# Packing the two parities of a projection as 128 + 64 columns, in a four-layer convolution and scan kernel

## The chip, the cores and the metric

The kernel runs on one core of one Trainium2 chip. The metric is device time in microseconds (us) of one execution. Engines are named as in the profile: PE is TensorE's matrix unit and PEld its weight loads, DVE is VectorE, ACT is ScalarE, POOL is GpSimd, and SP is SyncE, which only issues DMAs.

## The reference

64 images of 96 channels and 28 x 28 pixels go through four layers in float32. Layer 0 is an inverted residual block whose kernels are mixed from four experts by routing weights of the image, with a squeeze-and-excite gate; layers 1 and 3 are plain inverted residual blocks; layer 2 is a selective scan over four quadrants of the image.

```python
# layer 0
rw = softmax(relu(pool @ r_w1.T + r_b1) @ r_w2.T + r_b2)
out = silu(_bn(einsum('oc,bchw->bohw', exp_w, x), ...))            # 96 -> 576 channels
out = silu(_bn(_dwconv_per_sample(out, einsum('be,eckl->bckl', rw, dw_w)), ...))   # 5 x 5
sc = sigmoid(silu(out.mean(axis=(2, 3)) @ se_w1.T + se_b1) @ se_w2.T + se_b2)
out = out * sc[:, :, None, None]
out = einsum('boc,bchw->bohw', einsum('be,eoc->boc', rw, pw_w), out)   # 576 -> 96
x = x + _bn(out, ...)
# layers 1 and 3
out = relu(_bn(_conv(x, w1), ...))                                 # 96 -> 576
out = relu(_bn(_conv(out, wd, stride=1, padding=1, groups=M), ...))    # 3 x 3
x = _bn(_conv(out, w3), ...) + x                                   # 576 -> 96
# layer 2, for each of four quadrants: norm, 1x1 conv, 3x3 depthwise conv, then four scans
h = dA * h + (d_t * u_t)[..., None] * B_t[:, :, None, :]           # 196 steps
y_t = einsum('bdcn,bdn->bdc', h, C_t)
```

## The kernel before

**Stages.** In the steady part four images are in work: one in layer 2 (`mamba`), the others in layers 1, 0 and 3 (`convs`). `slot` sets up one step of this pipeline for each image, `opening` and the end of `mk_conv_seq_kernel` the ramps.

**A convolution block** has three parts. `expand` (L725, L755) multiplies the image by 4.5 blocks of 128 hidden channels; ScalarE evicts each bank into one of two padded tiles, `border` (L709), and stores it in HBM (`ex`). `load` fetches shifted rows of `ex` into `rep`, with SyncE's DMAs, and builds or fetches the taps `wd`. `depthwise` (L835) does the depthwise convolution on PE as a small matmul per column offset, in column tiles of 32; a partition of its result holds one hidden channel at one parity of the image row: 4 blocks x 2 parities x 16 channels, so 64 hidden channels on 128 partitions. ScalarE evicts it into an `acc` tile of 128 partitions and 392 elements (14 row pairs x 28), L845. A projection needs nine `acc` tiles ("groups") for 576 channels.

**`project`** (L872) multiplies the nine `acc` tiles by the projection weights. An `acc` tile holds both row parities on its partitions, so the weights of parity `o` are zero on the partitions of the other parity: for each group, two matmuls of 128 partitions x 96 columns run over the same 392 elements, one into each of two PSUM banks. VectorE adds bias and residual (L876). For layers 1 and 3 the weights are constants (`w3` in the blob); for layer 0 `squeeze_excite` mixes them on PE (L969) and VectorE multiplies them by the gate into `wp` (L994), once for each parity. Nine groups are three operations of six matmuls each.

**Layer 2.** `head` normalises a half image (`group_norm`: statistics on VectorE, small matmuls L1075, L1071 and L1072 on PE, small operations on ScalarE and GpSimd), then shifted matmuls (L1119), taps (L1141) and two 1x1 convolutions (L1162, L1173). `scans` does, for each of 12 scan pairs of an image, on ScalarE the decays (L1269) and a copy of the inputs into `du` (L1279), on VectorE two products (L1291) and two scans in each direction (L1296, L1301), on GpSimd four sums and products (L1248). L1223 sums the states on PE. `tail` normalises, gates and adds.

**The order.** Nothing runs when it is written down: `Plan.op` records each operation with its engine, an estimated cost, what it reads and writes and a due time. `Plan.run` simulates the engines and, on each, always takes the candidate of the earliest due time among those that could start first; an operation may start at most `AHEAD` (45 us) before its due time. The due time is a position on a time axis on which one image takes `T` = 145 us, plus a correction from the table `DUE` for each kind of operation. The instructions are then emitted in that order, and each engine works strictly in it. Where the plan sees PE idle so long that its clock would fall, `idle` puts filler matmuls on zeros (L539) ahead of the next one. The pools (`POOLS`) hold 4 PSUM banks `ps`, 12 `acc` tiles and one `du`.

Of the kernel before, what the change touches and what calls it, by code (L numbers as in the profile page):

```python
# [10 lines left out]
AF = mybir.ActivationFunctionType  # L11
# [143 lines left out]
def pack_l1(ins, layer):  # L155
# [12 lines left out]
    out = np.zeros((4, 2, CB, 2, NG, C), np.float32)  # L168
    for o in range(2):
        out[:, o, :, o] = w3.reshape(4, 2, CB, NG, C)[:, o]  # L170
    p.add("w3", out.reshape(P, 2 * NG, C))
# [4 lines left out]
def pack_l2(ins):  # L176
# [41 lines left out]
PE, ACT, DVE, POOL, SP = "PE", "ACT", "DVE", "POOL", "SP"  # L218
EXP, PLUS, SILU = "exp", "plus", "silu"
# [11 lines left out]
    71, -2, 48, -17, 58, 181, 21, -12, 9, -37, -2, 21, 37, -23, 1, -16, 19, -12, 30, -17, 33, -40, 12, -8, -30, -60,  # L231
    -12, 9, 0, -16, 16, -56, 115, 47, -23, -9, 16, 45, -29, 63, -28, 34, 12, 35, 43, 2, -32, -7, 21, -7, 6, 14, 37,
    13, -22, 36, -19, 13, -27, 7, -23, -17, 130, -19, 113, 50, 16, 35, 28, 2, 22, 11, -45, 12, -30, 30, -30, -13, -6,
    -6, -12, -8, -7, 20, 24, 117, 11, 25, -20, 15, -13, 1, 51, 43, 29, 147, 47, 40, -10, -15, -7, 10, 30, -10, 20,
    129, 8, 11, 31,
# [17 lines left out]
class Plan:  # L253
# [4 lines left out]
    AHEAD = 45.0  # L258

    HOP = {PE: 1.0, DVE: 0.6, ACT: 0.4, POOL: 0.4, SP: 0.2}  # L260
    LAND = 0.7
    ALONE = 130e3
    RATE = 300e3
    TABLE = 1.28
    ANY_ORDER = ("ps", "gs")
    WARM, WINDOW = 0.7, 3.4
    GRACE = {PE: 0.3, ACT: 0.2, DVE: 0.25, POOL: 0.25, SP: 0.0}
# [10 lines left out]
    def op(self, engine, cost, fn, r=(), w=(), due=None, table=None, nbytes=0, after=(), land=None, lock=False):  # L278
        o = Op()
        o.engine, o.cost, o.fn, o.table, o.nbytes = engine, cost, fn, table, nbytes  # L280
        o.land, o.lock = land, lock or engine == POOL
        kind = self.k.kinds.setdefault((fn.__code__, self.tag), len(self.k.kinds))
        o.due = (self.due if due is None else due) + (DUE[kind] if kind < len(DUE) else 0.0)
# [39 lines left out]
    def run(self, start=0.0):  # L323
# [3 lines left out]
        table, dma, left, lock, ahead = None, start, len(self.ops), start, None  # L327
        used = []
# [18 lines left out]
        while left:  # L347
            best = None
            for e, q in queue.items():
# [16 lines left out]
                key = lambda c: (c[1].due + (8.0 if c[1].table and c[1].table != table else 0.0), c[1].n)  # L366
# [9 lines left out]
            if o.table and o.table != table:  # L376
                cost += self.TABLE
                table = o.table
# [11 lines left out]
            o.behind = None  # L390
# [7 lines left out]
            if o.nbytes:  # L398

                dma = max(dma, t + 0.5) + o.nbytes / self.RATE  # L400
                end = max(dma + 1.5, t + cost + (o.land or 2.0 + o.nbytes / self.ALONE)) + self.LAND
# [6 lines left out]
            for b in set(o.bufs):  # L408
                b.left -= 1
                b.end = max(b.end, end + 0.2)  # L410
            for d, data in o.out:
                d.wait -= 1
                if data:
                    d.ready = max(d.ready, end + (self.HOP[d.engine] if d.engine != e or o.nbytes else 0.0))
                if not d.wait:
                    queue[d.engine].append(d)
# [56 lines left out]
class Kernel:  # L473
    T = 145.0
# [13 lines left out]
        wp=(1, [P, 2, NG, C]),  # L488
# [90 lines left out]
    def fold_bn3(self, row, w3):  # L579

        k = w3.shape[1]
        self.nc.vector.tensor_tensor(w3, w3, row.rearrange("p (a o) -> p a o", a=1).to_broadcast([P, k, C]), ALU.mult)
# [12 lines left out]
    def setup(self, fold, banks):  # L595
# [22 lines left out]
        for layer, c in ((1, c1), (3, c3)):  # L618
# [4 lines left out]
            self.fold_bn3(self.row_of(banks, s3, eye, f"fold_row{layer}"), c("w3"))  # L623
# [75 lines left out]
    def expand(self, d):  # L699
# [17 lines left out]
        for t in range(4):  # L717
# [3 lines left out]
            for h in range(2):  # L721
                ps = pl.buf("ps")

                def mm(ps=ps, t=t, h=h):
# [4 lines left out]
                pl.op(PE, 0.72, mm, r=d["keys"], w=[ps], after=[("pad", i, h)])  # L729
                pl.op(  # L730
                    ACT, 0.68, lambda ps=ps, t=t, h=h, pad=pad: evict(pad[:, :, 1 + 7 * h : 8 + 7 * h, 2:30], ps, t),
# [38 lines left out]
        pl.op(PE, 0.81, mm, r=d["keys"], w=[ps], after=["hpad"])  # L770
        pl.op(ACT, 0.68, lambda: evict(pad[:, :, :, 2:30], ps, 4), r=[ps], w=["hpad"], table=d["table"])
# [14 lines left out]
    def load(self, d, u):  # L786
# [18 lines left out]
        if layer == 0:  # L805
            pl.op(POOL, 1.3, spread, r=[d["kern"]], w=[wd])
# [713 lines left out]
```

## Time and profile before

| what | value |
|---|---|
| median of 3 runs | 9315.91 us (9309.75 to 9317.01) |
| the profiled execution | 9312.17 us |
| its span | 9310.4 us |
| mean granted PE clock | 0.965 |
| ACT busy | 6345.8 us |
| POOL busy | 6778.1 us |
| DMA moved | 2029.93 MB, mean 218 GB/s |

The profile's groups name the line, the engine, the operation, the tile that is written and those that are read; behind "x" is the count, then come the busy time in us, the mean time of one in ns, and the idle time of the engine just before them with what ended it. "128*96" ahead of a shape is rows by columns of the PE array that a matmul uses. A float32 matmul is recorded as two matmuls and two weight loads. PE's matmuls are pipelined, so the time of one in a run is read from start to start.

### The profile page before, as it was taken

What the parts mean: (1) busy time and instruction counts of PE and PEld (TensorE: products, weight loads), DVE (VectorE), ACT (ScalarE), POOL (GpSimd) and SP (SyncE); (2) the same over time, 40 slices, a digit from 0 to 9 for tenths busy, and PEclk for the clock granted to TensorE, in tenths of its full rate; (3) what the DMA queues carried; (4) which work ended last, traced back from release to release, by engine and by line L of the source; (5) the groups of instructions that cost most, each with busy time, mean ns of one, the idle gap of its engine ahead of it and who ended that gap; (6) DMA issues with size and microseconds to landing.
All of it is one profiled execution on the core that took longest, in us unless ns stands there. A gap on an engine that the chain in (4) does not pass through costs nothing. (4 is left out here: it accounts for less than half of the span.)

```text
span 9310.4 us, 198515 instructions
## 1 busy us (share of the span) xinstructions
PE 8870.7 (95%) x78114; PEld 4120.6 (44%) x78114; DVE 7772.0 (83%) x7806; ACT 6345.8 (68%) x10934; POOL 6778.1 (73%) x4445
## 2 busy tenths in 40 slices
PE   7899999999999999999999999999999999999997
PEld 3344444444444444444444444444444444444443
DVE  1888888888888888888888888888888888888886
ACT  3667767767667677667677676676676676776763
POOL 2777777777777777777777777777777777777775
PEclk9899999999999999999999999999999999999998
DMA  6688888888888888888888888888888888888884
GB/s 174 185 213 231 223 220 225 227 222 220 224 226 219 221 229 221 215 229 224 219 225 227 223 222 225 224 220 222 228 221 222 227 222 215 230 223 220 225 227 105
DMA packets 1063983, 2029.93 MB, mean 218 GB/s; under 512 B 114065, under 2 KB 890001, under 8 KB 1062673
## 3 DMA queue, kind: packets, MB, share of 16 engines
q1 hardware_dynamic: 810576, 1520.44, 66.6%
q10 hardware_dynamic: 252480, 496.79, 15.4%
q8 instruction: 624, 10.22, 0.5%
q14 instruction: 303, 2.47, 0.1%
HBM read 1499.83 MB, written 516.95 MB: 217 GB/s over the span
## 5 line engine op out<-in xcount | busy, mean ns | idle before, releaser
L835 PE MATMUL ps<-rep,wd 64*32 64x392 f32 (+1 forms) x50688 | 3609.0, 521 | 38.8 <-DMA rep<-ex 14.9
L1301 DVE TENSOR_TENSOR_SCAN g<-decay,b 128x788 f32<-128x788 f32 x1536 | 2755.1, 1794 | 324.8 <-ACT decay L1269 190.1
L1296 DVE TENSOR_TENSOR_SCAN h<-decay,b 128x788 f32<-128x788 f32 x1536 | 2721.4, 1772 | 0.0
L835 PEld LDWEIGHTS ps<-rep,wd 64*32 64x32 f32 (+1 forms) x50688 | 1491.4, 110 | 1822.9 <-issue 1596.4
L1248 POOL TENSOR_TENSOR yc<-h,g 128x784 f32<-128x784 f32 x768 | 1436.9, 1871 | 1095.9 <-DVE h L1296 657.6
L1291 DVE TENSOR_TENSOR b<-du,B 128x784 f32<-128x784 f32 x1536 | 1505.0, 980 | 675.9 <-ACT du L1279 605.8
L845 ACT ACTIVATE acc<-ps,l_bn2b,l_bn2s 128x392 f32<-128x392 f32 x1728 | 1124.2, 674 | 1338.1 <-PE ps L835 1311.3
L1248 POOL TENSOR_TENSOR g<-h,g 128x784 f32<-128x784 f32 x768 | 1425.7, 1856 | 801.4 <-DVE h L1296 800.6
L872 PE MATMUL ps<-acc,blob 128*96 128x392 f32 x4608 | 1602.3, 498 | 4.7
L1248 POOL TENSOR_TENSOR yc<-yc,C 128x784 f32<-128x784 f32 x768 | 1426.5, 1857 | 55.2
L1269 ACT ACTIVATE decay<-dd,A 128x784 f32<-128x784 f32 x1536 | 1372.5, 943 | 38.0 <-DVE h L1296 14.4
L1248 POOL TENSOR_TENSOR yc<-yc,g 128x784 f32<-128x784 f32 x768 | 1318.1, 1716 | 45.9
L725 PE MATMUL ps<-x,blob 96*128 96x392 f32 x3072 | 1186.5, 518 | 22.3 <-ACT border L709 9.5
L709 ACT ACTIVATE border<-ps,l_bn1b,l_bn1s 128x392 f32<-128x392 f32 x1536 | 976.0, 677 | 220.0 <-DMA ex<-border 109.1
L872 PEld LDWEIGHTS ps<-acc,blob 128*96 128x96 f32 x4608 | 725.8, 163 | 755.8 <-issue 635.3
L588 POOL TENSOR_TENSOR wd<-kern,blob 96x640 f32<-96x640 f32 x576 | 753.6, 1317 | 163.1 <-PE ps L835 85.1
L1269 ACT ACT_TABLE_LOAD x439 | 563.2, 1283 | 334.7 <-issue 178.6
L725 PEld LDWEIGHTS ps<-x,blob 96*128 96x128 f32 x3072 | 536.7, 191 | 547.5 <-ACT acc L845 79.7
L872 PE MATMUL ps<-acc,wp 128*96 128x392 f32 x2304 | 771.8, 493 | 0.6 <-ACT a L1166 0.6
L872 PEld LDWEIGHTS ps<-acc,wp 128*96 128x96 f32 x2304 | 376.4, 163 | 383.7 <-issue 373.6
L1279 ACT COPY du<-dd 128x392 f32<-128x392 f32 x768 | 374.2, 487 | 219.0 <-DVE b L1291 124.3
L1223 PE MATMUL y<-yc,blob 128*32 128x392 f32 x3072 | 398.1, 502 | 29.8 <-POOL yc L1248 29.8
(144 smaller groups left out, 6599.8 us busy)
## 6 DMA issues: line engine op xcount, KB each, us to landing
rep<-ex SPq DMA_DIRECT2D x4032, 224.0 KB, 5.1
ex<-border ACTq DMA_DIRECT2D x512, 480.0 KB, 5.5
dd<-ddd SPq DMA_DIRECT2D x384, 588.0 KB, 7.2
ex<-border ACTq DMA_DIRECT2D x256, 512.0 KB, 5.1
B<-bcd SPq DMA_DIRECT2D x256, 392.0 KB, 4.3
C<-bcd SPq DMA_DIRECT2D x256, 392.0 KB, 4.8
wd<-taps SPq DMA_DIRECT2D x512, 192.0 KB, 6.7
ddd<-dd ACTq DMA_DIRECT2D x128, 441.0 KB, 3.5
```

The lines of the kernel that those rows point to most:

```text
L588: self.nc.gpsimd.tensor_tensor(out, taps.rearrange("k (n a) -> k n a", a=1).to_broadcast([k, n, cb]), mask.rearrange("k (a c) -> k a c", a ...
L709: nc.scalar.activation(dst, ps()[:, :HALF].rearrange("p (r o w) -> p o r w", o=2, w=28), d["func"], bias=bias[:, t : t + 1], scale=scale[: ...
L725: nc.tensor.matmul(ps()[:, :HALF], w1[:, t * P : t * P + P], x[:, h * HALF : (h + 1) * HALF], start=True, stop=True)
L835: nc.tensor.matmul(ps()[32 * b : 32 * b + 32, :HALF], wd()[64 * h : 64 * h + lanes, at : at + 2 * CB], rep()[64 * h : 64 * h + lanes, b, : ...
L845: nc.scalar.activation(acc(), ps()[:, :HALF], d["func"], bias=bias[:, at : at + 1], scale=scale[:, at : at + 1], **kw)
L872: nc.tensor.matmul(banks[o]()[:C, :HALF], w, a, start=(g == 0), stop=(g == NG - 1))
L1223: nc.tensor.matmul(y()[32 * j : 32 * j + 32, :HALF], c("sel"), ys[j]()[:, 2 * u : 2 * u + 2], start=(k == 0 and u == 0), stop=(k == 1 and ...
L1248: nc.gpsimd.tensor_tensor(*vs, op)
L1269: nc.scalar.activation(fs[:, :, u, :, :SEQ], d()[:, :2].rearrange("p o (i l) -> p o i l", i=2), AF.Exp, scale=self.A[:, at : at + 1],)
L1291: nc.vector.tensor_tensor(out, v, w, ALU.mult)
L1296: lambda h=h, ff=ff: nc.vector.tensor_tensor_scan(flat(h()), ff, b, 0.0, ALU.mult, ALU.add),
L1301: lambda g=g, ff=ff: nc.vector.tensor_tensor_scan(flat(g())[:, ::-1], ff[:, ::-1], b[:, ::-1], 0.0, ALU.mult, ALU.add),
```

## The change

**Weights.** Of each group, the 96 columns of parity 0 and 32 columns (channels 64 to 95) of parity 1 are packed side by side into 128 columns; the other 64 columns of parity 1 (channels 0 to 63) form a second part. `w3` and `wp` have the shape [128, 9, 192] now, in place of [128, 18, 96] and [128, 2, 9, 96].

**Matmuls.** Three groups give one operation of three 128-column matmuls over 392 elements into bank 0, and one operation of six matmuls of 64 columns over 196 elements into bank 1: the lower 64 array columns take the first half of the elements, the upper 64 the second half.

**Additions.** The two additions become four, after both parts: parity 0 (96 partitions), channels 64 to 95 of parity 1 (32 partitions), and twice 64 partitions by 196 elements. The gate of layer 0 and the setup's fold of the scale are split in the same way.

**The plan.** PE's operations have a form, `FULL` or `TILED`; a change of form costs `MODE` (0.1 us) in the plan and counts 0.5 in the choice among candidates. `AHEAD` goes from 45 to 500, `T` from 145 to 134, `DUE` is a new table, many estimated costs are a little lower, times are rounded to 1/256 us, and a small lag after an operation (`LAG`) is counted.

```diff
@@ pack_l1
-    out = np.zeros((4, 2, CB, 2, NG, C), np.float32)
-    for o in range(2):
-        out[:, o, :, o] = w3.reshape(4, 2, CB, NG, C)[:, o]
-    p.add("w3", out.reshape(P, 2 * NG, C))
+    w3 = w3.reshape(4, 2, CB, NG, C)
+    out = np.zeros((4, 2, CB, NG, 2 * C), np.float32)
+    out[:, 0, :, :, :C] = w3[:, 0]
+    out[:, 1, :, :, C:P] = w3[:, 1, :, :, 64:]
+    out[:, 1, :, :, P:] = w3[:, 1, :, :, :64]
+    p.add("w3", out.reshape(P, NG, 2 * C))
@@ Plan
-    AHEAD = 45.0
+    AHEAD = 500.0
+    LAG = {PE: 0.0, DVE: tick(0.1), ACT: tick(0.1), POOL: tick(0.05), SP: 0.0}
-    TABLE = 1.28
+    TABLE, MODE = tick(1.28), tick(0.1)
+    MODE_PEN = 0.5
@@ Plan.op
+        o.table = table or (FULL if engine == PE else None)
@@ Plan.run
-                key = lambda c: (c[1].due + (8.0 if c[1].table and c[1].table != table else 0.0), c[1].n)
+                other = lambda o: o.table and o.table != (mode if o.engine == PE else table)
+                key = lambda c: (c[1].due + (self.MODE_PEN if e == PE else 8.0) * bool(other(c[1])), c[1].n)
...
-            if o.table and o.table != table:
-                cost += self.TABLE
-                table = o.table
+            if other(o):
+                if e == PE:
+                    cost += self.MODE
+                    mode = o.table
+                else:
+                    cost += self.TABLE
+                    table = o.table
@@ Kernel
-    T = 145.0
+    T = 134.0
-        wp=(1, [P, 2, NG, C]),
+        wp=(1, [P, NG, 2 * C]),
@@ setup
-            self.fold_bn3(self.row_of(banks, s3, eye, f"fold_row{layer}"), c("w3"))
+            row = self.row_of(banks, s3, eye, f"fold_row{layer}")
+            for lo, hi, out in ((0, C, 0), (64, C, C), (0, 64, P)):
+                self.fold_bn3(row[:, lo:hi], c("w3")[:, :, out : out + hi - lo])
@@ depthwise
-        pl.op(PE, 0.69 * k, mm, r=[rep, wd], w=[*banks, *accs])
+        pl.op(PE, 0.67 * k, mm, r=[rep, wd], w=[*banks, *accs], table=TILED)
@@ project
-        def mm(lo):
+        def mm(half, lo):
             for g in range(lo, lo + 3):
-                for o in range(2):
-                    w, a = terms(o, g)
-                    nc.tensor.matmul(banks[o]()[:C, :HALF], w, a, start=(g == 0), stop=(g == NG - 1))
-
-        def add(o):
-            xs = d["x"].rearrange("c (r o w) -> c o r w", o=2, w=28)[:, o]
+                w, a, kw = weights()[:, g], accs[g](), dict(start=(g == 0), stop=(g == NG - 1))
+                if half == 0:
+                    nc.tensor.matmul(banks[0]()[:, :HALF], w[:, :P], a, **kw)
+                    continue
+                for h in range(2):
+                    nc.tensor.matmul(
+                        banks[1]()[64 * h : 64 * h + 64, :SEQ], w[:, P:], a[:, h * SEQ : h * SEQ + SEQ], **kw
+                    )
+
+        xs = lambda o: d["x"].rearrange("c (r o w) -> c o r w", o=2, w=28)[:, o]
+
+        def add(x, ps, lo, hi):
             nc.vector.scalar_tensor_tensor(
-                xs, banks[o]()[:C, :HALF].rearrange("c (r w) -> c r w", w=28), d["b3"], xs, ALU.add, ALU.add
+                x, ps.rearrange("c (r w) -> c r w", w=28), d["b3"][lo:hi], x, ALU.add, ALU.add
             )
 
+        def first():
+            add(xs(0), banks[0]()[:C, :HALF], 0, C)
+            add(xs(1)[64:], banks[0]()[C:, :HALF], 64, C)
+
+        def second():
+            for h in range(2):
+                add(xs(1)[:64, 7 * h : 7 * h + 7], banks[1]()[64 * h : 64 * h + 64, :SEQ], 0, 64)
+
         for lo in range(0, NG, 3):
-            pl.op(PE, 0.67 * 6, lambda lo=lo: mm(lo), r=[*(accs[lo : lo + 3] if lo else accs), wp], w=banks)
-        for o in range(2):
-            pl.op(DVE, 0.65, lambda o=o: add(o), r=[banks[o], *d["keys"]], w=d["keys"])
+            ready = [*(accs[lo : lo + 3] if lo else accs), wp]
+            pl.op(PE, 1.97, lambda lo=lo: mm(0, lo), r=ready, w=[banks[0]])
+            pl.op(PE, 1.27, lambda lo=lo: mm(1, lo), r=ready, w=[banks[1]], table=TILED)
+        pl.op(DVE, 1.3, first, r=[banks[0], *d["keys"]], w=d["keys"])
+        pl.op(DVE, 0.78, second, r=[banks[1], *d["keys"]], w=d["keys"])
@@ squeeze_excite
+            def gated(o, lo=lo, hi=hi, acc=acc):
+                for a, b, out in ((0, C, 0),) if o == 0 else ((64, C, C), (0, 64, P)):
+                    v = sc()[:, o * NG + lo : o * NG + hi].rearrange("p (g a) -> p g a", a=1)
+                    nc.vector.tensor_tensor(
+                        wp()[:, lo:hi, out : out + b - a], acc()[:, :, a:b], v.to_broadcast([P, hi - lo, b - a]), ALU.mult
+                    )
```

## The prediction

> **What bounds the kernel now.** I read the page first, then one image's stretch by windows, then TensorE's timeline inside it.
>
> The page, with its groups of instructions:
>
> ```profile
> span 9310.4 us, 198515 instructions
> ...
> PE 8870.7 (95%) x78114; PEld 4120.6 (44%) x78114; DVE 7772.0 (83%) x7806; ACT 6345.8 (68%) x10934; POOL 6778.1 (73%) x4445
> ...
> L872 PE MATMUL ps<-acc,blob 128*96 128x392 f32 x4608 | 1602.3, 498 | 4.7
> ...
> L872 PE MATMUL ps<-acc,wp 128*96 128x392 f32 x2304 | 771.8, 493 | 0.6 <-ACT a L1166 0.6
> ```
>
> PE is busy 95% of the span, and the projections (L872) are a quarter of that. A float32 matmul leaves two records, so 4608 + 2304 records are 3456 matmuls: 192 projections (64 images, three layers) of 9 groups and 2 parities.
>
> One image by windows (length; busy time of PE, PEld, DVE, ACT, POOL; granted clock; DMA share; GB/s):
>
> ```profile
> 4000.00:4141.00 141.00, 136.09 (x1213) 63.30 (x1215) 119.10 (x117) 98.56 (x171) 104.10 (x70) 0.96 0.84 221
> 4052.00:4057.00 5.00, 0.77 (x4) 0.39 (x2) 3.25 (x2) 2.81 (x4) 0.00 (x0) 0.89 0.63 226
> 4057.00:4070.00 13.00, 12.90 (x135) 7.66 (x134) 9.95 (x12) 8.66 (x20) 9.96 (x9) 0.65 0.89 235
> ```
>
> PE works 136 of 141 us, VectorE (DVE) 119. The five missing us stand in one place, 4052 to 4057, and the 13 us after it run at a clock of 0.65. TensorE's timeline (start, length, group) shows the place, and the prices that I use:
>
> ```profile
> 4025.34 2.17 PE L1141 MATMUL ps<-p,blob 128*32 128x196 f32 x36
> 4027.43 0.90 PE L1162 MATMUL ps<-hn,blob 96*96 96x392 f32 x2
> ...
> 4029.02 12.02 PE L872 MATMUL ps<-acc,wp 128*96 128x392 f32 x36
> 4040.97 4.27 PE L835 MATMUL ps<-rep,wd 64*32 64x392 f32 x96
> 4045.17 2.90 PE L725 MATMUL ps<-x,blob 96*128 96x392 f32 x8
> 4048.00 1.52 PE L1223 MATMUL y<-yc,blob 128*32 128x392 f32 x12
> 4049.45 2.90 PE L725 MATMUL ps<-x,blob 96*128 96x392 f32 x8
> 4056.58 0.48 PE L1075 MATMUL ps<-gs,blob 96*96 96x2 f32 x2 [4.23 <-ACT border L709]
> ...
> 4098.13 0.88 PE L755 MATMUL ps<-x,blob 96*64 96x392 f32 x4
> 4098.94 2.96 PE L725 MATMUL ps<-x,blob 96*128 96x392 f32 x8
> ```
>
> A burst of eight expansions (L725) fills the banks, ScalarE cannot evict into `border`, and the small L1075 stands for 4.23 us. The table of waits (total, times, longest) gives its total, and VectorE's longest wait; the page's chain of waits covers the last 100 us alone, so I leave it:
>
> ```profile
> DVE b L1291 <- ACT du L1279: 605.8, 181, 14.0
> ...
> PE ps L1075 <- ACT border L709: 226.8, 61, 5.4
> ```
>
> The stall comes 61 times in 64 images. With the mean clock of 0.965, at most 0.035 x 9310.4 = 326 us of PE time is lost to the low clock; the stall and what follows it are worth up to 226.8 + 326 = 553 us.
>
> **The projection itself.** Removed: 3456 full-height matmuls of 96 columns. One costs (4040.97 - 4029.02) / 18 = 0.664 us, so 2295 us. Added: 1728 matmuls of 128 columns over the same 392 elements, and 1728 pairs of 64-column tiles, each over 196. The first stream as many elements and cost 0.664: 1147 us. L725 has 128 columns: 4 in 4048.00 - 4045.17 = 2.83, 0.708 each with the edges of so short a run in it; that is the upper bound (1223 us). For the pair the nearest row is L1141: three column tiles side by side, 196 elements, six rounds in 4027.43 - 4025.34 = 2.09 us, 0.348 a round. Two tiles abreast for the same stream: 1728 x 0.348 = 601 us. That tiles of 64 columns run side by side is shown by L755: two matmuls over 392 from 4098.13 to 4098.94, 0.81 us, where one after the other would take 1.33.
>
> Bounds of the pair: half a full matmul, 0.332, from below; from above its four weight loads one behind the other. L755's loads have a median of 136 ns, so 0.544 a pair, 940 us. I take 0.348, because L1141 issues 36 loads of 109 ns, 3.9 us in all, within its 2.09, so loads do overlap.
>
> [...]
>
> **Changes of array form.** In the order of the built programs, changes between full width, 64 and 32 columns go from 2440 to 2809. Price: L755's 0.81 less 0.664, shared by entering and leaving, 0.073; 369 x 0.073 = 27 us. Bounds 0 and 0.146 (54 us).
>
> Sum of this part: 2295 - 1147 - 601 - 27 = 520 us less; between 78 (2295 - 1223 - 940 - 54) and 574 (2295 - 1147 - 574).
>
> **VectorE's part.** Two additions of 96x392 (L876, 226.6 us over 384, some 0.6 each) become four: 96x392, 32x392 (as many elements a partition, so again 0.6) and two of 64x196, for which the nearest rows are L1358 (0.345) and L1380 (0.404). That is +0.74 x 192 = 142 us. Gating the mixed weights splits two of four operations; a small one, L980, takes 0.167: 0.167 x 2 x 64 = 21 us. VectorE goes to 7772 + 163 = 7935 us. I cost this at nothing: it has 1538 us of idle time now, and 8700 - 7935 = 765 would be left. Were VectorE the bound, the 163 would count in full. The three folds in the setup are a few us, before the steady part.
>
> **The order.** Costs, due times, the look-ahead (45 to 500) and the period (145 to 134) change nothing on an engine but its order. DMA issues on SyncE stay 5720, and ScalarE's table loads fall by 55 (17 to 16 an image), 55 x 1.283 = 71 us on an engine with 3000 us idle: nothing. What is moved:
>
> 1. The projections are cut: nine full matmuls, other work, then pairs. The `acc` tiles stay held until the last pair, and both additions come behind it; the next expansion is late by at most the work placed between.
> 2. The burst before L1075 is gone: its successor (L1109) now follows 36 depthwise matmuls and one expansion, and the other seven of that image are spread between parts of a projection. On ScalarE the evictions into `border` still go two tiles, two stores, then a `decay`, then again two tiles, so a wait for the store can stay there; what is queued behind it are the normalisation (L1345) and, for VectorE, `du`. So the 553 us may go wholly, or stay.
> 3. Filler matmuls (L539) go from 75 to 328, 31,282 to 112,312 columns; at 0.664 / 392 each, 137 us more, most of it before the shifted matmuls (L1119), where the new order leaves PE waiting for `hn`. If the wait is real they are a new wait of that size; if not, they delay PE by it. I count 137 either way; the bounds are 0 and 137.
>
> Of the 553 I take 230. More than this meets VectorE: in its 141 us it idles 21.9, and by its timeline five waits between 4041 and 4066, around the stall, (5.30 for `du`, 1.65 for `y`, 2.43 for a decay, 1.85 for `du`, 0.80) are 12.0 of these. With them gone an image needs 119.1 + 163 / 64 + 9.9 = 131.5 us on VectorE, 9.5 less: 9310.4 - 64 x 9.5 = 8702.
>
> Sum: 9310.4 - 520 - 230 + 137 = 8697. The profiled execution itself took 9312.2 and the median of the runs is 9315.9, 5.5 above the span: some 8700 us.
>
> **Rivals.**
>
> A. The stall stays whole, moved to another eviction. For it: ScalarE's pattern above, with 5.1 to 5.5 us from a store's issue to its landing by the page's DMA issues. Against: no burst before L1109. 9310.4 - 520 + 5.5 = 8796; with the fillers as a delay 8933.
>
> B. The 64-column pairs are bound by their loads. For it: no row here runs 64-column tiles over 196 elements. Against: L1141. With every upper bound 9310.4 - 78 + 5.5 = 9238; with the loads alone (940, 27: 181 us less) 9135.
>
> C. Slower: the retuned order misfits the chip. One mechanism: ScalarE works in order, a `du` copy stands behind an eviction that waits for PE, VectorE's product L1291 then waits (605.8 us now), banks stay full, PE stands over two us and its clock halves. Each such stall costs what the present one does, (226.8 + 326) / 61 = 9.1 us. The 520 are gone at 57 more stalls, about one an image; two an image give 9316 - 520 + 128 x 9.1 = 9961. Against it: ScalarE waits 1311 us for L835 already, and little of that reaches PE.
>
> D. The stall goes entirely and VectorE's other waits shrink with it: 9310.4 - 520 - 553 + 137 + 5.5 = 8380, to 8560 with a third of the 553 left.
>
> E. The packing gains nothing because something else paces the image: between 9297 and 9335. Against it: PE's 97% inside an image.
>
> **How the numbers follow.** Forecast (8560 to 8760) 0.50; A (8760 to 8940) 0.24; D 0.12; B 0.05; C 0.07; E 0.02. The predicted time is the forecast's, 8700. The range runs from 8450 (half of D) to 8900 (nearly all of A, down to bounds of the pair): outside are half of D, B, C, E and a rest of A, 0.20 or slightly more. About 0.2% is what a measurement of this kernel tells from no change: faster 0.91, same 0.02, slower 0.07.
>
> **What would show it.** In the changed profile: full projection matmuls at 0.66 us each and pairs near 0.35 (three in 1.0 to 1.2); PE's idle time before L1109 and the low-clock stretches fewer than 61; VectorE busy some 7935; waits before the shifted matmuls (then L1153), where the fillers are. Pairs over 0.5, a mean clock below 0.965, or VectorE's wait for `du` over 605 us would prove me wrong, and say which of B, A or C it is.

## The result, and the profile after

| | time, us (median, range) | ratio to before | profiled span, us | mean granted clock |
|---|---|---|---|---|
| before | 9314.98 (9309.75 to 9317.01) | | 9310.4 | 0.965 |
| changed | 9378.93 (9370.38 to 9396.84) | 1.0072 [1.0055, 1.0089] | 9368.6 | 0.95 |

The change makes the kernel 0.7% slower. Predicted were 8700 us, 8450 to 8900; the time lies outside, 679 us above the forecast.

Line numbers move: L855 is the depthwise matmul (L835 before), L891 and L894 the two parts of the projection (L872), L901 its additions (L876), L745 the expansion (L725), L1109 the small matmul of `group_norm` at which PE stood before (L1075), L1313 and L1325 `du` and the product (L1279, L1291), L802 and L829 SyncE's loads of rows and taps.

The page of the changed kernel:

```profile
span 9368.6 us, 206587 instructions
...
PE 8609.7 (92%) x82076; PEld 4215.2 (45%) x82076; DVE 7962.5 (85%) x8322; ACT 6288.4 (67%) x10879; POOL 6772.4 (72%) x4445
...
L855 PE MATMUL ps<-rep,wd 64*32 64x392 f32 (+1 forms) x50688 | 3617.4, 517 | 510.7 <-DMA wd<-taps 396.1
...
L891 PE MATMUL ps<-acc,blob 128*128 128x392 f32 x2304 | 796.9, 495 | 0.0
L901 DVE SCALAR_TENSOR_TENSOR x<-ps,l_bn3b,x 64x196 f32<-64x196 f32 (+2 forms) x768 | 397.7, 518 | 385.2 <-PE ps L891 370.3
...
L894 PE MATMUL ps<-acc,blob 128*64 128x196 f32 x4608 | 424.9, 333 | 0.9
```

PE is busy for 261 us less, and the span is 58 us longer. The projection is not what waits (0.0 and 0.9 us idle before it); the depthwise matmuls stand for their taps. The table of waits (total, times, longest) says the same:

```profile
PE ps L855 <- DMA wd<-taps: 396.1, 65, 8.1
DVE x L901 <- PE ps L891: 370.3, 67, 42.7
...
DVE b L1325 <- ACT du L1313: 222.1, 92, 6.7
...
DVE rw L927 <- DMA x<-x_dram: 183.2, 59, 4.9
```

The stall before L1109 is gone, as forecast, and VectorE's wait for `du` fell from 605.8 to 222.1 us. In their place stands one wait of some 6 us an image for a DMA that SyncE issues. TensorE's timeline around it (start, length, group):

```profile
4088.76 4.80 PE L855 MATMUL ps<-rep,wd 64*32 64x392 f32 x96
4099.68 4.26 PE L855 MATMUL ps<-rep,wd 64*32 64x392 f32 x48 [6.13 <-DMA wd<-taps]
...
4110.85 6.09 PE L891 MATMUL ps<-acc,blob 128*128 128x392 f32 x18
4116.87 0.88 PE L775 MATMUL ps<-x,blob 96*64 96x392 f32 x4
...
4121.44 3.21 PE L894 MATMUL ps<-acc,blob 128*64 128x196 f32 x36
4124.58 2.24 PE L745 MATMUL ps<-x,blob 96*128 96x392 f32 x6
```

and the same place by windows (length; busy time of PE, PEld, DVE, ACT, POOL; clock; DMA share; GB/s):

```profile
4094.00:4099.60 5.60, 0.00 (x0) 0.00 (x0) 4.14 (x3) 0.90 (x2) 5.44 (x4) 0.76 0.98 235
4099.60:4104.00 4.40, 4.32 (x49) 2.00 (x50) 3.03 (x3) 0.00 (x0) 0.38 (x1) 0.53 1.06 237
```

PE stands for 6.13 us, and the 48 records behind (two for each matmul) take 4.26 us, where 96 took 4.80 ahead of it: the clock is 0.53. Nine full matmuls take 4116.87 - 4110.85 = 6.02 us, 0.669 each, and nine pairs 4124.58 - 4121.44 = 3.14 us, 0.349 each: the packing itself is as fast as forecast.

Over 40 images of the steady part (from one start of layer 0's pooling sum to the next) this is, in us an image; "low" is PE's busy time at half clock (the trace has 0.50 there), of which half is counted as lost:

| | period | PE idle | low | stretches of low clock | rest: PE's work at full clock |
|---|---|---|---|---|---|
| before | 141.51 | 4.80 | 7.71 | 1.00 | 141.51 - 4.80 - 3.86 = 132.85 |
| changed | 142.26 | 9.72 | 9.88 | 1.80 | 142.26 - 9.72 - 4.94 = 127.60 |

So 5.25 us of work an image are gone (some 8.5 of the projection, less 3.0 of fillers), and 4.92 of idle time and 1.08 of low clock came: +0.75. PE's work fell as expected, and PE spends the time waiting.

Why SyncE is late, from the trace's records of single DMA issues (start, line, tiles, landing):

```
4088.75 SP   L802  rep<-ex   landed 4092.76
4090.45 ACT  L1212 bcd<-bc   landed 4092.94
4092.95 SP   L802  rep<-ex   landed 4096.31, released 4092.94 by the landing of bcd<-bc
4094.53 SP   L829  wd<-taps  landed 4099.55
4099.68 PE   L855  first matmul of the unit
```

SyncE's row load has nothing to do with ScalarE's store `bcd`. But in these programs the DMAs of both queues share eight semaphores: in the trace of the changed kernel each of the eight is used by 709 to 722 DMAs of SyncE and by 169 to 182 of ScalarE. They are handed out in turn: from one DMA of SyncE to the next the semaphore goes on by one in 4692 of 5716 steps, and the others skip 1411 in all, where ScalarE has 1412 DMAs. Here ScalarE's store, which ScalarE reaches late (4090.45), and SyncE's load have the same semaphore, number 103, and the load waits for it: it starts 0.01 us after the store has landed. SyncE's own waits show the pair 119 times, each time with one semaphore for both:

```profile
SPq L802 <- DMA bcd<-bc: 638.5, 119, 7.9
```

### The profile page after: what moved, and what is told of

Its sections match the earlier page's. It is cut to its first block, busy times and chain, and to the rows that moved or that the text cites. A ratio compares the mean times of both kernels' runs of the same rounds, so it can differ in the third digit from the quotient of the medians.

```text
span 9368.6 us, 206587 instructions
## 1 busy us (share of the span) xinstructions
PE 8609.7 (92%) x82076; PEld 4215.2 (45%) x82076; DVE 7962.5 (85%) x8322; ACT 6288.4 (67%) x10879; POOL 6772.4 (72%) x4445
## 5 line engine op out<-in xcount | busy, mean ns | idle before, releaser
L855 PE MATMUL ps<-rep,wd 64*32 64x392 f32 (+1 forms) x50688 | 3617.4, 517 | 510.7 <-DMA wd<-taps 396.1
L855 PEld LDWEIGHTS ps<-rep,wd 64*32 64x32 f32 (+1 forms) x50688 | 1456.5, 109 | 2281.5 <-issue 1985.4
L1325 DVE TENSOR_TENSOR b<-du,B 128x784 f32<-128x784 f32 x1536 | 1509.6, 983 | 323.6 <-ACT du L1313 222.1
L1303 ACT ACTIVATE decay<-dd,A 128x784 f32<-128x784 f32 x1536 | 1353.1, 941 | 226.7 <-DVE h L1330 217.2
L745 PE MATMUL ps<-x,blob 96*128 96x392 f32 x3072 | 1290.6, 538 | 78.1 <-ACT acc L865 52.9
L729 ACT ACTIVATE border<-ps,l_bn1b,l_bn1s 128x392 f32<-128x392 f32 x1536 | 989.1, 674 | 328.4 <-PE ps L745 220.5
L745 PEld LDWEIGHTS ps<-x,blob 96*128 96x128 f32 x3072 | 538.9, 196 | 575.9 <-issue 129.1
L891 PE MATMUL ps<-acc,blob 128*128 128x392 f32 x2304 | 796.9, 495 | 0.0
L901 DVE SCALAR_TENSOR_TENSOR x<-ps,l_bn3b,x 64x196 f32<-64x196 f32 (+2 forms) x768 | 397.7, 518 | 385.2 <-PE ps L891 370.3
L1313 ACT COPY du<-dd 128x392 f32<-128x392 f32 x768 | 376.7, 491 | 480.0 <-DVE b L1325 459.1
L891 PEld LDWEIGHTS ps<-acc,blob 128*128 128x128 f32 x2304 | 433.6, 190 | 304.0 <-issue 2.6
L1257 PE MATMUL y<-yc,blob 128*32 128x392 f32 x3072 | 420.3, 505 | 47.0 <-POOL yc L1282 47.0
L894 PE MATMUL ps<-acc,blob 128*64 128x196 f32 x4608 | 424.9, 333 | 0.9
```

The costliest lines, as they stand in the source:

```text
L729: nc.scalar.activation(dst, ps()[:, :HALF].rearrange("p (r o w) -> p o r w", o=2, w=28), d["func"], bias=bias[:, t : t + 1], scale=scale[: ...
L745: nc.tensor.matmul(ps()[:, :HALF], w1[:, t * P : t * P + P], x[:, h * HALF : (h + 1) * HALF], start=True, stop=True)
L855: nc.tensor.matmul(ps()[32 * b : 32 * b + 32, :HALF], wd()[64 * h : 64 * h + lanes, at : at + 2 * CB], rep()[64 * h : 64 * h + lanes, b, : ...
L891: nc.tensor.matmul(banks[0]()[:, :HALF], w[:, :P], a, **kw)
L894: nc.tensor.matmul(banks[1]()[64 * h : 64 * h + 64, :SEQ], w[:, P:], a[:, h * SEQ : h * SEQ + SEQ], **kw)
L1303: nc.scalar.activation(fs[:, :, u, :, :SEQ], d()[:, :2].rearrange("p o (i l) -> p o i l", i=2), AF.Exp, scale=self.A[:, at : at + 1],)
```

## The experiments

All times are medians; the kernel before took 9299 to 9308 us beside them and 9315 beside the changed kernel, so a difference of some 16 us between two kernels that were not timed side by side means nothing. In e1, e2, e11 and e12, every engine's instructions and their order are those of the kernel they start from, and only the turn of the semaphores differs; the runs built on them add fillers or leave additions out, and nothing else.

### e1 and e2: DMA semaphores in the planned order

Each DMA is tied to the one before it in the plan, without a wait on the chip, so that the semaphores are handed out in the order in which the plan starts the DMAs. e1 is the changed kernel, e2 the kernel before.

```diff
             last[e] = o.last = i
+            if type(i).__name__ == "InstDMACopy":
+                if self.dma:
+                    self.k.tc.add_manual_dep(i, self.dma.name, NoSync, reason="lane")
+                self.dma = i
```

> The changed kernel, every engine's instructions in the same order; only the order in which DMAs of SyncE and ScalarE take the eight shared DMA semaphores is now that of the plan, so that SyncE's row loads of layer 1 no longer take a semaphore that ScalarE's later store of bcd holds. Theory (shared semaphore): the changed kernel lost its gain in one stall an image, PE waiting 6.5 us for wd<-taps, because SyncE stands 4.5 us for the bcd store. Then SyncE's wait for bcd at the row loads (638 us, 119 times) falls below 150, PE's wait for wd<-taps (396 us) below 150, the mean clock rises from 0.95 to 0.97 or more, and the time falls to 8800 to 9050. Rival (pace): VectorE and its coupling with ScalarE pace the image at 141 us whatever PE does; the wait for taps shrinks but PE's idle time comes back elsewhere: 9300 to 9400.

> The kernel before with the same edit of the semaphore order. Theory (shared semaphore): its stall, L1075 behind the burst of expansions, is not one of SyncE's, so little changes: 9200 to 9400, PE's wait at L1075 still 150 to 300 us. Rival (pace): the same, 9250 to 9350. If it falls below 9100, the shared semaphores cost the kernel before as much as the changed one, and the difference between the two needs another cause.

e1: 9265.44 us, ratio 0.9962 [0.9947, 0.9976]; e2: 9206.92 us, 0.9898 [0.9883, 0.9913]. So the semaphores cost the changed kernel 114 us and the kernel before 92: nearly the same, so they are not what makes the one slower than the other. With the semaphores in order in both, the change still costs 9265 - 9207 = 58 us. In e1 SyncE's row loads no longer wait for `bcd` at all, and PE's wait for the taps falls from 396.1 to 101.4 us; but other waits of the depthwise matmuls grow (those for "issue" from 20.5 us, for POOL's `wd` from 13.7):

```profile
PE ps L864 <- DMA wd<-taps: 101.4, 46, 4.6
PE ps L864 <- issue: 65.0, 37, 3.1
PE ps L754 <- ACT acc L874: 46.4, 59, 1.3
...
PE ps L864 <- POOL wd L615: 42.8, 32, 2.2
PE ps L864 <- DVE x L910: 41.3, 59, 1.0
```

PE still idles 7.11 us an image, and its low clock stays (12.03 busy in 1.68 stretches). The theory that this wait was all (8800 to 9050) is refuted; it was only the largest of several. The rival's time (9300 to 9400) was not met either, but what it said of the idle time, that it comes back elsewhere, was so in part.

e2 lies in the theory's range, but not for its reason. Its stall behind the burst of expansions was to stay at 150 to 300 us; it fell from 226.8 to 122.1 (L1084 in e2, L1075 before). So about half of the wait that the prediction put down to the burst and ScalarE's evictions went with the semaphores. Over the same 40 images e2 has a period of 139.77 us, PE idle for 3.47 and 6.38 busy at low clock.

### e3 and e4: the packing alone, the order alone

e3 has the plan of the kernel before and its operations; each projection operation issues three full matmuls and three pairs, with the split additions, gate and folds. e4 has the new order with the old two matmuls of 96 columns.

```diff
 e3, on the kernel before
+        def both(lo):
+            mm(0, lo)
+            mm(1, lo)
...
-            pl.op(PE, 0.67 * 6, lambda lo=lo: mm(lo), ...)
+            pl.op(PE, 0.67 * 6, lambda lo=lo: both(lo), ...)
```

> The packing alone: the kernel before with every planned operation where it was (costs, due times, look-ahead of before), but a planned projection operation issues three 128-column matmuls and three pairs of 64 columns in place of six of 96, and additions, gate and folds are split. Theory (shared semaphore): the packing is worth its 520 us where the order does not take it back, and the stall at L1075 stays: 8750 to 8900. Rival (pace): VectorE paces the image, PE's saving becomes idle time: 9250 to 9350. Rival (pairs): the pairs are bound by their weight loads, over 0.5 us each: 9100 to 9300.

> The new order alone: the changed kernel's plan, operation by operation, but a planned projection operation issues three matmuls of 96 columns into one bank, so that the old 3456 matmuls are done; additions, gate and folds as before. Theory (shared semaphore): the order loses some 560 us against the old one with the same work, so the time is 9750 to 9950, with the wait for wd<-taps still there (250 to 450 us). Rival (pace): the added 520 us of PE work fit into PE's idle time, 9380 to 9500.

e3: 9691.92 us, 1.0411 [1.0393, 1.0428], clock 0.923; e4: 9771.54 us, 1.0516 [1.0492, 1.0539]. For e3 the theory and both rivals said far less than was measured; e4 is where the theory put it. Each part alone costs 4 to 5%. On the old order the packing loses 393 us; on the new one it gains 9772 - 9379 = 393. PE's waits in e3 (L1095 is the small matmul, L729 the expansion, L839 the depthwise matmul):

```profile
PE ps L1095 <- ACT border L713: 353.6, 61, 7.4
PE ps L729 <- DVE x L885: 190.9, 62, 3.5
PE ps L729 <- DVE rw L942: 75.7, 60, 1.6
PE ps L839 <- DVE x L885: 52.1, 60, 1.2
```

PE is through with the projection earlier and stands at the banks that VectorE's additions (L885) have still to free, 190.9 us before L729 and 52.1 before L839; the mean clock is 0.923, and the old stall for `border` grows from 226.8 to 353.6 us.

### e5: the saved time filled again, on the old order

```diff
         def both(lo):
+            nc.tensor.matmul(banks[0]()[:, :HALF], <128x128 zeros>, <128x392 zeros>,
+                start=(lo == 0), stop=(lo == 0))
             mm(0, lo)
```

> The packed projection on the old order (the run that took 9691.92 us), with one useless matmul of 128 columns over 392 zeros (0.66 us) ahead of each of the 576 thirds: PE's saved time is filled again, 576 x 0.664 = 382 us of work. Theory (what PE saves becomes idle time at the banks and at the evictions, and each stand of 2 us or more halves its clock after it): PE arrives at the fixed hand-offs as late as in the kernel before, the waits for VectorE's additions (159 + 64 us) and for border (296 us) fall to about those of before, the clock goes back towards 0.96, and the time falls, to 9300 to 9450, although PE does more work. Rival (VectorE's four additions hold the banks and pace the image): the time stays at 9650 to 9750. Rival (PE's work itself sets the time): 9692 + 382 = 10074.

9577.21 us, 1.0294 [1.0278, 1.0309]: 382 us of useless work make e3 115 us faster; the clock goes from 0.923 to 0.944 and PE's idle time from 11.79 to 7.38 us an image. The direction is the theory's, the size is not: 274 us over the kernel before remain. Neither rival's time came; how much the additions do cost is asked in e6 and e7.

### e6 and e7: VectorE's additions, on the old order

e6 is the kernel before with only its two additions cut into four. e7 is e3 without two of the four, so that its output lacks those parts.

```diff
 e6, on the kernel before
+        def first():
+            add(xs(0), banks[0]()[:C, :HALF], 0, C)
+            add(xs(1)[64:], banks[1]()[64:C, :HALF], 64, C)
+
+        def second():
+            for h in range(2):
+                add(xs(1)[:64, 7 * h : 7 * h + 7], banks[1]()[:64, SEQ * h : SEQ * h + SEQ], 0, 64)
```

> The kernel before with one edit: its two additions of a projection are cut into the four of the change (96x392, 32x392 and twice 64x196), the matmuls, gate and order as before. VectorE has 192 x (0.63 + 2 x 0.42 - 0.61) = 165 us more. Theory (the loss of the packing on the old order is idle time and low clock of a PE that is too early): little, 9300 to 9440 with the additions' 165 us at most partly on the path. Rival (the longer additions, behind which the banks stay held, are the cost): most of the 393 us that the packing lost on this order, 9600 to 9700.

> The packed projection on the old order with two of its four additions left out (the 32x392 and one of 64x196, so channels 64 to 95 of one parity and half of its others lack the projection in the output): VectorE has slightly less to do than in the kernel before. Theory: PE still comes early to the banks and to border, the time stays above 9500. Rival (the additions are the cost): the loss of 393 us goes, and PE's 520 us show, 9300 or less.

e6: 9487.20 us, 1.0192 [1.0175, 1.0209]. e7: 9506.20 us, 1.0213 [1.0197, 1.0228]. The additions cost 9487 - 9303 = 184 us with the old matmuls and 9692 - 9506 = 186 with the packed ones, about the 165 to 202 us by which they are longer: on this order they count in full, although VectorE idles 20 us an image. The other half of e3's loss, some 203 us, is there without them. That it is PE, early at its hand-offs, is likely from e5, where holding PE back took 115 us off, but no run shows it for the whole. Neither theory holds alone.

### e8: no fillers in the changed kernel

```diff
-            self.k.idle(o.target(), o.fill)
+            pass
```

> The changed kernel without its filler matmuls (the planned order is the same). Prediction's step: they cost 0 to 137 us. Theory (PE waits for hn there anyway, and the fillers keep its clock up): the wait shows at the shifted matmuls as idle time, some 3 us an image, and at least as many low stretches follow: 9379 to 9500. Rival (the fillers delay PE): 9190 to 9300, up to 190 us less.

9409.52 us, 1.0111 [1.0096, 1.0126], 31 us slower than with them, as the theory had it. All 328 are left out, the 75 that the kernel before has among them. The wait for `hn` that they cover shows:

```profile
PE ps L855 <- DMA wd<-taps: 397.8, 65, 7.8
PE ps L1153 <- ACT hn L1141: 112.7, 62, 5.2
```

The stretches of low clock rise from 1.80 to 2.77 an image.

### e9 and e10: the stall filled, and two additions left out, on the new order

e9 is the changed kernel with 5 us of fillers ahead of the unit that stalls; e10 is the changed kernel without two of its four additions (its output lacks those parts).

```diff
 e9
         def mm():
+            if d["layer"] == 1 and u == 3:
+                self.idle(banks[0](), 5.0)
```

> The changed kernel with 5.0 us of useless matmuls on zeros ahead of one depthwise unit of each image, the one that waits some 6.5 us for its taps (344 us of wait in the steady part). 64 x 5.0 = 320 us more work for PE. Theory (the wait is late SyncE, not PE, and after it the clock is half for 7 to 10 us, about 3.4 us of work lost an image): the wait shrinks below 2 us, a low stretch an image goes, and the time falls by 64 x 3.4 = 218 us at most, to 9160 to 9300, although PE does more. Rival (another engine paces the image, the clock costs nothing): 9350 to 9400. Rival (PE's work sets the time): 9379 + 320 = 9700.

> The changed kernel with two of a projection's four additions left out (the 32x392 and one of 64x196; the output lacks those parts). VectorE has 192 x (0.63 + 0.42) = 202 us less, some 39 us less than with two additions of the kernel before. If the additions count in full on this order as they do on the old one (184 and 186 us there): 9379 - 190 = 9190. If VectorE's waits hide them, as the prediction had it: 9340 to 9380.

e9: 9343.11 us, 1.0039 [1.0024, 1.0054]: 320 us more work, 36 us less time; the stretch of low clock after the stall goes (1.80 to 0.95 an image, clock 0.965). That is far less than the 218 us at most, and the time lies between the theory's range and that of the rival by which the clock costs nothing. SyncE is held as before (its row loads wait 633.2 us for `bcd`, 638.5 in the changed kernel), and the fillers stand where the wait stood: PE idles 4.54 us an image in place of 9.72, and its work rises by 5.4. What is gained is low clock, and less of it than hoped: the image's other stretch grew (from 7.5 to 8.8 us in the mean), so that PE's low busy time fell only from 9.88 to 8.21 us an image. e10: 9356.73 us, 1.0047 [1.0030, 1.0064], 22 us less, which is hardly clear of noise (the intervals overlap): on this order the additions are nearly hidden, as the prediction had it. VectorE has only more to wait: its wait for the image's own load (L927 in the changed kernel), which SyncE issues too, is 295.5 us in e10 and 183.2 in the changed kernel.

### e11 and e12: semaphores in order, with the order alone and with the packing alone

e11 is e4, e12 is e3, with the edit of e1.

> The new order with the old matmuls (the run that took 9771.54 us), with the DMA semaphores taken in the planned order. The order alone cost 472 us. Theory (a good part of that is SyncE, held by ScalarE's late store through a shared semaphore, 233 us of PE's wait for the taps and the low clock after it): 9400 to 9600. Rival (the order itself misfits, through ScalarE's and VectorE's fixed turns): 9650 to 9770, the lane edit is worth 90 to 115 us as in the two kernels where it was tried.

> The packed projection on the old order (9691.92 us) with the DMA semaphores taken in the planned order. Its waits are for VectorE's additions (159 + 64 us) and for border (296 us), which are evictions behind stores; SyncE's are few. Theory (the old order's loss is the late release of PSUM banks by VectorE and the low clock after it, not SyncE): 9500 to 9620, as much gained as in the kernel before (92 us) or up to twice that. Rival (the semaphores are behind this loss too): 9150 to 9300.

e11: 9363.56 us, 1.0067 [1.0042, 1.0092]; e12: 9579.56 us, 1.0299 [1.0283, 1.0315]. The order by itself cost 472 us; 408 of these go with the semaphores, and 57 over the kernel before are left. The like pair is e2, which has them in order too: over it 157 are left, so the semaphores are 315 of the 472. The packing on the old order still loses 373 us against e2; its loss has another cause (e5 to e7). e12 is where the theory put it. e11 is below the theory's 9400 to 9600: the semaphores were behind more of it than the wait for the taps showed.

### e13 to e16: PE's clock, with the semaphores in order

In e1 one stretch of half clock an image begins where no wait is above 1 us. By windows, e1, before it and in it:

```profile
4122.70:4126.10 3.40, 2.66 (x31) 2.23 (x23) 3.19 (x4) 3.28 (x9) 3.32 (x3) 1.00 0.78 216
4126.10:4143.30 17.20, 16.52 (x62) 7.72 (x65) 10.08 (x12) 5.21 (x12) 14.40 (x10) 0.50 0.93 293
```

These 3.4 us hold a wait of 0.74 us and the small matmuls of `squeeze_excite`, 18 records over one column each, some 1.5 us; then the clock is 0.50 for 17.2 us. e13 is e1 with fillers ahead of those and of the next small ones; e15 has fillers ahead of the unit that waits for its taps too; e16 is e13 with the old matmuls; e14 is e1 without two of the four additions.

```diff
 e13
         def squeeze():
+            self.idle(ps(), 1.3)
...
         def excite():
+            self.idle(ps(), 0.7)
 e15, besides
         def mm():
+            if d["layer"] == 1 and u == 3:
+                self.idle(banks[0](), 2.0)
```

> The changed kernel with the DMA semaphores in the planned order (9265.44 us), and 1.3 + 0.7 us of useless matmuls on zeros ahead of the two groups of very small matmuls of squeeze_excite, where in 39 of 40 images a low-clock stretch of 9.1 us begins with a gap of only 0.8 us before it: 64 x 2.0 = 128 us more work. Theory (the gate sees the small matmuls as idle time, and the half clock costs 64 x 4.5 = 290 us): that stretch goes from most images, 9090 to 9200. Rival (another engine paces the image): 9255 to 9290. Rival (PE's work sets the time): 9393.

> The changed kernel with the DMA semaphores in the planned order (9265.44 us), with two of a projection's four additions left out (the 32x392 and one of 64x196; the output lacks those parts), 202 us less on VectorE. Theory (PE's low clock and its small waits hold the time, VectorE has slack): 9230 to 9265. Rival (with SyncE out of the way VectorE, busy 124 of 141 us an image, paces the image, and the additions that the prediction costed at nothing count): 9060 to 9120.

> The kernel of e13 with 2.0 us of useless matmuls also ahead of the depthwise unit that waits for its taps (90 us of wait in the steady part, 42 times, and 10 of 40 images have a low stretch of 3.8 us after it): 128 us more work again. Theory: about as e13, between 60 us less (where the wait is there anyway) and 60 us more: 9050 to 9260. Rival (PE's work sets the time): 9520.

> The new order with the old matmuls and the DMA semaphores in the planned order (9363.56 us), with the same 1.3 + 0.7 us of useless matmuls at squeeze_excite as in the packed kernel that took 9175.85 us. Theory (PE is nearly always busy here, 3.1 us idle and 7.2 us of low clock in 142 an image, and 35 of 39 low stretches begin at squeeze_excite): the clock is worth 64 x 3.5 = 224 us and the useless work costs 128, so 9260 to 9330, and the packing is worth 85 to 155 us here, the rest of its 520 being idle time at waits of 0.7 to 2 us for other engines. Rival (with the clock kept up the packing shows in full): 9176 + 520 = 9696, or at least 9450.

e13: 9175.85 us, 0.9864 [0.9849, 0.9879]. e14: 9269.63 us, 0.9965 [0.9950, 0.9980], no gain over e1: VectorE's additions don't hold the image here. e15: 9119.68 us, 0.9801 [0.9784, 0.9817], **2.0% faster than the kernel before, and the fastest of all**. Half of that is the semaphores' order, which gives the kernel before 1.0% too (e2); e15 is 87 us below e2, and no run gives e2 fillers at those places. e16: 9308.60 us, 1.0014 [1.0002, 1.0025]. e13, e15 and e16 are where the theory put them, e14 is 5 us above its range and far from the rival's. The same two windows in e15:

```profile
4122.70:4126.10 3.40, 3.40 (x12) 2.00 (x11) 3.19 (x3) 2.15 (x3) 1.96 (x2) 1.00 0.91 264
4126.10:4143.30 17.20, 16.30 (x192) 8.58 (x198) 16.81 (x20) 12.51 (x22) 12.98 (x8) 1.00 1.00 254
```

The two kernels are at different points of an image there; over 40 images, PE's low busy time is 12.03 us an image in e1, 5.49 in e13 and 3.27 in e15.

The times together:

| | old matmuls | packed | packing |
|---|---|---|---|
| old order | 9299 | 9692 | +393 |
| old order, semaphores in order | 9207 | 9580 | +373 |
| new order | 9772 | 9379 | -393 |
| new order, semaphores in order | 9364 | 9265 | -98 |
| the same, fillers at `squeeze_excite` | 9309 | 9176 | -133 |
| the same, fillers at the taps too | | 9120 | |

## Why the prediction was wrong

**The projection, 520 us.** The size was right: 0.669 and 0.349 us, against 0.664 and 0.348. Three pairs in a row take 1.15 us, 0.38 each with the edges. Per image PE's busy time for the projection falls from 36.55 to 28.0 us, 8.5 x 64 = 547 us. What failed is the step from PE's work to the time, which the sum takes as one to one. In the cleanest pair of runs, e16 and e13, the saved work is 7.6 us an image (137.5 less 129.9 at full clock), and it splits into 1.7 of a shorter period, 3.8 of more idle time (6.71 against 2.90) and 2.1 of half clock (5.49 against 1.37, halved). A quarter arrives.

**"Of the 553 I take 230."** This step failed most. The stall at L1075 went, as said. But idle time and half clock together rose from (4.80 + 3.86) x 64 = 554 to (9.72 + 4.94) x 64 = 938 us: plus 384 in place of minus 230. That is 614 of the 679 us by which the forecast missed. Nor was the place chosen well: about half of the wait at L1075 goes with the semaphores alone (e2), with the burst of expansions left as it was.

**"The order ... change nothing on an engine but its order. DMA issues on SyncE stay 5720".** The sum has the order as a gain of 230 - 137 = 93 us. With the old matmuls it costs 472 (e4), and on top of it the packing gains 393 of its 520: 565 and 127 us off, together about the miss. (The split hangs on which part comes first: on the old order the packing costs 393, and the new order then takes 313 off.) The count of SyncE's issues was right, their turn wasn't looked at. The move changed which DMA shares a semaphore with which, and a late store of ScalarE came to stand in front of SyncE's row loads; with the old matmuls that is 315 of the 472 us (e2, e4, e11).

For the packed kernel the semaphores are not the whole cause, and not the cause of the sign. Put in order they give it 114 of the 679 us, the kernel before gains 92 by the same, and 58 us of loss stay (e1, e2). With them in order PE's idle time and half clock still rise by the change, from 3.47 + 3.19 to 7.11 + 6.02 us an image, 414 us in all. Fillers win back 146 us of the changed kernel's time at two of the places (e13, e15). What holds the other engines' turns at 139 us an image there is not shown. The trace of before had a hint: SyncE waited 348.2 us for `bcd` at its loads of the taps there (L809). The list of "what is moved" followed ScalarE's evictions and PE's banks, and never SyncE's own waits.

**The fillers, +137, bounds 0 to 137.** Wrong in sign: without any of them the kernel is 31 us slower (e8). They take some 190 us of PE, but cover a wait of 113 us and low clock (2.77 stretches an image without them, 1.80 with).

**VectorE's part, costed at nothing.** About right on the new order: 22 us at most (e10), none with the semaphores in order (e14). Its busy time is 7962.5 us, 7935 were forecast. On the old order the step would have been wrong by 184 us (e6): 20 us of idle time an image did not hide the longer additions there.

**Form changes and table loads.** Nothing speaks against their small prices; neither was tried by itself.

**The rivals.** A's size for the stall (all of it stays, 8796 to 8933) was nearer than the forecast, but it took the stall as staying at an eviction. C is the one that came true in kind: the retuned order misfits, PE stands over two us about once an image and its clock halves, and the 520 are gone. By the traces between 1500 and 8500 us, each of the 49 waits of 2.0 to 5.4 us in the kernel before and of the 49 of 5.4 to 8.0 us in the changed one has a stretch at 0.50 that begins 2.1 to 5.3 us after the wait does. Its place was wrong: not ScalarE's `du`, whose wait fell, but PE's wait for taps that SyncE loads late. It had 0.07. Of the three signs named for a failure one came: the mean clock fell below 0.965, to 0.95. Pairs over 0.5 us and a longer wait for `du`, the sign of C, did not.

**What stays open.** The fastest packed kernel, e15, still takes 420 us more than the forecast, although PE idles 4.95 us of its 138.74 an image and VectorE is busy for 124 of them: what sets its period isn't shown, only that it isn't VectorE's additions in e1 (e14). The old order with the semaphores in order and fillers wasn't run, so what the packing is worth there with fillers isn't known. Why the packing gains 393 us on the new order as changed and only 98 with the semaphores in order isn't shown; SyncE's loads wait for PE's depthwise matmuls too (975.2 us at L802 and 828.7 at L829 in the changed kernel), so a faster PE may pull SyncE forward, but no run separates this. That the rest of the loss on the old order (e5, 274 us) is the additions and the split gate is likely from e6, not shown.

## What to carry to other kernels

Where several engines work in fixed turns, a cheaper operation may be worth only what the next hand-off can take (a quarter of it here, e16 and e13): count idle time and half-clock time before and after beside the work, and ask of each queue, SyncE's above all, what an issue waits for when the order moves. Semaphores shared between DMA queues were such a hand-off here (638.5 us of SyncE's waits in the changed kernel), and handing them out in the order in which the plan starts the DMAs gave 1 to 4% here, with no instruction moved. Try such a remedy on the kernel before as well: here it gained nearly as much there, which told that it was not what separated the two. Useless matmuls at the places where the clock falls can pay: 256 us of them took 146 us off the time.

## What was not expected of the hardware

- A stretch of low clock came without a long wait. In e1, 3.4 us with PE busy for 2.66, much of it matmuls over one column, are followed by 17.2 us at 0.50. In the changed kernel, between 1500 and 8500 us, 38 stretches begin with no wait above 1.3 us in the 3.4 us ahead of them, 30 of these with none above 0.15; in those 30 cases 20 to 25 of the 24 to 29 matmuls recorded there have one to four columns of data (2605.30 to 2608.70: busy for 3.40, clock 1.00; then 13.7 us at 0.50). That such matmuls count as idle time is e13's theory; the runs show that low clock follows them and, where fillers went ahead of them, that PE's low busy time fell from 12.03 to 5.49 us an image. In e8 waits of 1.7 us in the mean are followed by half clock in 32 of 40 images.
- After the wait of 6.5 us in the changed kernel the half clock lasts 6.8 us in the mean; the stretches come in steps of 3.4 us (in e1 3.4, 6.8, 10.2, 13.7 and 17.1; in the changed kernel 3.4, 6.8, 10.2 and 13.7 for 123 of 127).
- More work made a kernel faster four times: by 115 us (e5), 36 (e9), 90 (e13) and 56 (e15).
- Two tiles of 64 columns abreast run at 0.349 us a pair, about half a full matmul (0.669). Their four weight loads (136 ns each in e3's groups, 0.544 a pair) would take longer one behind the other, so they overlap here.
